# A vision tower in one kernel: zero writes moved behind the pixel transposes, weight means taken off TensorE, and q formed transposed in the linear attention

## The chip, the core and the metric

The kernel runs on one core of a Trainium2 chip. The metric is the device time of one execution in microseconds (us). A core has TensorE (PE, with PEld for its weight loads), VectorE (DVE), ScalarE (ACT), GpSimd (POOL) and SyncE (SP); SP, ACT and POOL issue DMAs.

## The reference

Four images of 3 x 224 x 224 are cut into patches of 8 x 8, 784 per image, each a row of 192 values. A tokenizer and two layers follow, all in fp32 with rows of 256 values:

```python
# tokenizer
tokens = layernorm(patches, ln1_g, ln1_b) @ W1 + b1
tokens = layernorm(tokens, ln2_g, ln2_b)
tokens = concatenate([tokens, tokens, tokens], axis=1)       # 3 x 784 tokens
h1 = silu(layernorm(tokens @ Wp1 + bp1, lnp_g, lnp_b)); h = h1 @ Wp2 + bp2
# layer 0: attention over the images, then 6 experts, the best two of each token
# layer 1: linear attention on x = layernorm(h)
qkv = x @ W_qkv + b_qkv; q, k, v = split(qkv, 3)
q = q - mean(q); k = k - mean(k)
q2 = q*q; k2 = k*k
k2 = l2_normalize(k2 / (sum(k2) + 1e-7), axis=tokens)
q2 = l2_normalize(q2 / (sum(q2) + 1e-7), axis=channels)
kv = einsum('bnc,bnd->bcd', k2, v)
h = h + (v + einsum('bnc,bcd->bnd', q2, kv) / sqrt(N)) @ W_out + b_out
# then 4 small experts and a shared one, the best two of each token
```

## The kernel before

The token rows come three times over, so the kernel works on 784 per image and writes each row three times: 28 tiles of 112 rows (`TT`) in all. h stays in SBUF. The tile framework places the waits; blocks in `tc.manual_schedule` keep the written order on the engines named there, elsewhere a scheduler orders the instructions of each engine. PSUM has seven rotating buffers (`ps_tile`).

**The front (L93 to L575).** DVE sets constants: base0, table, blk and shift for the placing of tokens on experts (L119 to L138, some 70 small memsets and an add), and zeros in the rows of img behind the pixels (L228). TensorE transposes table to tcol (L142). POOL issues the small loads (bp1, the rows of stage); SP and ACT issue W1, Wp1, the four images into img (L224) and the attention's weights. Then POOL clears `nothing` (L252) and SP writes it 40 times to the DRAM buffers xrows and yrows (L256), whose unused rows must be zero. Each hardware DMA takes one of eight semaphore slots in turn and waits for the slot's last user. `tok` is a pool that is closed after the tokenizer (L575); the memory of its tiles is used again by kq, mT and later by the experts' buffers, which wait for the last use of what lay there.

`first_layers` (L376) folds the weights: W1 times the first gain, less its mean over the 192 values of a patch (`without_mean`, L366: a product with a matrix of ones, then DVE), the bias row b1, both put in the order of the transposed pixels by `perm` and `srow` (L404, L408) to give Wall; then the same for Wp1 (W2), and the product of both (L422 to L437). For seven groups of four patch columns `patch_stds` (L440) forms variances on DVE and a root on ACT, which goes into img as a row behind the pixels, and `turn_patches` (L351) transposes pixels with 32 small products for each of two halves, copied to pT by ACT. A last product gives ev; the transposed stage gives cols (L503), the columns of all biases and gains. `first_rows` (L508, products at L517) and `tokenize` follow, then attention (L1086 on) and the experts of layer 0 (L1256 to L1506), whose blocks are read from xrows and written to yrows, with hb as hidden tile.

**The linear attention (L1380 to L1800).** A unit is 4 or 3 tiles of one image; there are eight. `centred_weights` (L623) takes the means out of the q and k columns of Wqkv. For unit u, `x_t` transposes the normalised rows to lxT, `q_k` (L1604) forms q and k of each tile together in a product of 512 columns, adds the bias on DVE (L1624), squares both on ACT in place with sums, and squares q again for the fourth powers (L1629). `scales` (L1637) forms both norms; q is scaled on DVE (L1653), k on ACT (uk). `fold` sums squares of uk. `q_t` (L1671) transposes q. `k_x` (L1676) forms uk^T x of an image, `g_t` and `kv_out` bring it to kvo. `rows_out` (L1728) adds x Wvo + q kvo to h, where Wvo is Wv W_out from `layer1_weights` (L639), called in unit 1 (L1780). Within `q_k`, `stats_one` and `normalise` prepare the rows of the next unit: they add the experts' rows (ys, gathered from yrows by POOL) to h and normalise it.

Of the kernel before, what the change touches and what calls it, by code (L numbers as in the profile page):

```python
# [37 lines left out]
CH = 3  # L38
# [22 lines left out]
def tile_vit_tower(ctx: ExitStack, tc: tile.TileContext, a: dict, out: bass.AP):  # L61
# [57 lines left out]
    base0 = const.tile([TT, E0], F32, tag="base0", name="base0")  # L119
    for e in range(E0):  # L120
        nc.vector.memset(base0[:, e : e + 1], float(CAP * e))


    NQ = QMAX * E0
    table = const.tile([1, 4, NQ], F32, tag="table", name="table")
    for q in range(QMAX):
        nc.vector.memset(table[:, 0, q * E0 : (q + 1) * E0], float(BLK * q))
    by_e = table.rearrange("r k (q e) -> r k q e", e=E0)
    for e in range(E0):
        for k, v in ((1, CAP * e - DUMMY), (2, EW * e), (3, D * e)):  # L130
            nc.vector.memset(by_e[:, k, :, e], float(v))
    nc.vector.tensor_tensor(table[:, 1, :], table[:, 0, :], table[:, 1, :], ALU.add)
    blk = const.tile([NQ, NBLK], F32, tag="blk", name="blk")
    for i in range(NBLK):
        nc.vector.memset(blk[:, i : i + 1], float(i))
    shift = const.tile([1, 3, NBLK], F32, tag="shift", name="shift")
    nc.vector.memset(shift, 0.0)
    nc.vector.memset(shift[:, 0, :], float(DUMMY))  # L138
    tcol = const.tile([NQ, 4], F32, tag="tcol", name="tcol")
    pt = ps_tile("ptable")  # L140
    for k in range(4):
        nc.tensor.transpose(pt[:NQ, k : k + 1], table[:, k, :], ident[:1, :1])  # L142
    nc.vector.tensor_copy(tcol, pt[:NQ, :4])

# [21 lines left out]
    tokp = tok.enter_context(tc.tile_pool(name="tok", bufs=1))  # L166
    bp1 = tokp.tile([TT, D], F32, tag="bp1", name="bp1")
# [39 lines left out]
    WID = HP * PATCH  # L207
    CY = CH * PATCH
    img = tokp.tile([TT, 32, WID], F32, tag="img", name="img")
# [18 lines left out]
    nc.vector.memset(img[:, CY:, :], 0.0)  # L228
# [22 lines left out]
    nothing = tokp.tile([P, 8 * D], F32, tag="nothing", name="nothing")  # L251
    nc.gpsimd.memset(nothing, 0.0)  # L252
    for r in range(0, XROWS, 8 * P):
        n = min(8, (XROWS - r) // P)
        for rows_ in (xrows, yrows):
            nc.sync.dma_start(  # L256
                out=rows_[r : r + n * P, :].rearrange("(p k) d -> p (k d)", k=n),
                in_=nothing[:, : n * D],
            )

# [86 lines left out]

    pT = tokp.tile([P, 2, NI * HP, HP], F32, tag="pT", name="pT")
# [17 lines left out]
    def without_mean(w, n, dim):  # L366

        pm = ps_tile("pmean")[:n, :D]
        for i in range(2):
            nc.tensor.matmul(pm, allones[:n, :n], w[:, i, :], start=(i == 0), stop=(i == 1))  # L370
        for i in range(2):
            nc.vector.scalar_tensor_tensor(
                w[:, i, :], pm, -1.0 / dim, w[:, i, :], ALU.mult, ALU.add
            )

    def first_layers():  # L376
# [14 lines left out]
        W2 = tokp.tile([P, 2, D], F32, tag="W2", name="W2")  # L391
        for i in range(2):
            nc.vector.tensor_scalar(W1g[:, i, :], W1[:, i, :], g1(i), None, ALU.mult)
        without_mean(W1g, KP, PD)
# [5 lines left out]
        nc.vector.tensor_tensor(b1, pw, b1, ALU.add)  # L400
# [10 lines left out]
        for c in range(2):  # L411
            nc.vector.tensor_scalar(W2[:, c, :], Wp1[:, c, :], g2(c), None, ALU.mult)
        for c in range(2):
            nc.vector.tensor_copy(
                bb[:, c, :], gb[:, 6 + c : 7 + c].to_broadcast([P, TT])
            )
        without_mean(W2, P, D)
# [8 lines left out]
        pw = ps_tile("pbw2")[:TT, :D]  # L426
        for c in range(2):
            nc.tensor.matmul(pw, bb[:, c, :], Wp1[:, c, :], start=(c == 0), stop=(c == 1))
        nc.vector.tensor_tensor(bp1, pw, bp1, ALU.add)
# [7 lines left out]
        nc.vector.tensor_copy(Wall[:, :, D:], pp)  # L437
        return Wall
# [42 lines left out]
    with tc.manual_schedule(engines={mybir.EngineType.DVE, mybir.EngineType.PE}):  # L481
        nc.vector.memset(srow, 0.0)
        nc.vector.memset(srow[:, SROW : SROW + 1], 1.0)
        nc.vector.memset(perm, 0.0)
        nc.vector.tensor_reduce(mod4, by4.rearrange("p j b -> p b j"), AX.X, ALU.add)
        nc.vector.tensor_reduce(div4, by4, AX.X, ALU.add)
        by_x = ident[:KP, :KP].rearrange("p (y x c) -> p x c y", x=PATCH, c=CH)
        for half in range(2):
            for i in range(2):
                nc.vector.tensor_copy(  # L490
                    perm[:, half, i, :, :CY].rearrange("p g (c y) -> p g c y", c=CH)[
                        :, :, :, 4 * half : 4 * (half + 1)
                    ],
                    by_x[:, 4 * i : 4 * (i + 1)],
                )
# [7 lines left out]
        nc.vector.tensor_copy(cols, pc[:, :nrows])  # L503
# [71 lines left out]
    tok.close()  # L575

# [62 lines left out]
    def layer1_weights():  # L639
# [8 lines left out]
        nc.vector.tensor_copy(WvT, pt)  # L648
        Wvo = w1p.tile([P, 2, D], F32, tag="Wvo", name="Wvo")
# [8 lines left out]
        bvs = w1p.tile([P, 2, P], F32, tag="bvs", name="bvs")  # L658
        for k in range(2):
            nc.vector.tensor_copy(bvs[:, k, :], col("bv", k).to_broadcast([P, P]))  # L660
# [724 lines left out]


# [35 lines left out]

    def stats_one(u, j):
# [4 lines left out]
        for k in range(2):  # L1428
            nc.vector.scalar_tensor_tensor(
                h[:, t, :], ys[u][:, j, k, :], wk[:, k, t : t + 1], h[:, t, :],  # L1430
                ALU.mult, ALU.add,
            )
        if j == 0:
            st = small.tile([TT, GT, 6], F32, tag="st", name="st")
            mv = small.tile([TT, GT, 2], F32, tag="mv", name="mv")
            stats[u] = st, mv
# [43 lines left out]
    with tc.manual_schedule(engines={mybir.EngineType.DVE, mybir.EngineType.SP}):  # L1480
        own_weights(NEARLY)
        turned(NEARLY)
        for i in range(NEARLY, NBLK + 1):
# [8 lines left out]
            if i == NEARLY + 1:  # L1492
                centred_weights()
            for u in range(3):
                if i - 1 == after[u]:
                    fetch(u)
# [105 lines left out]
    sumsof = {}  # L1602

    def q_k(u, j0, j1):  # L1604

        n = units[u][2]
        xT = xTs[u]
        if j0 == 0:
            qks[u] = lin.tile([TT, GT, 2 * D], F32, tag="qk", name="qk")
            sumsof[u] = (  # L1610
                small.tile([TT, GT, 2], F32, tag="ss", name="ss"),
                small.tile([TT, GT], F32, tag="s4", name="s4"),
            )
        qk = qks[u]
        ss, s4 = sumsof[u]
        junk = lin.tile([TT, D], F32, tag="junk", name="junk", bufs=1)
        for j in range(j0, min(j1, n)):
            pqk = ps_tile("pqk")[:TT]
            for c in range(2):
                nc.tensor.matmul(  # L1620
                    pqk, xT[:, c, cut(j, 1)], Wqkv[:, c, : 2 * D],
                    start=(c == 0), stop=(c == 1),
                )
            nc.vector.tensor_tensor(qk[:, j, :], pqk, bqkv[:, : 2 * D], ALU.add)  # L1624

            for i in range(2):
                half = qk[:, j, i * D : (i + 1) * D]
                nc.scalar.activation(half, half, AF.Square, accum_out=ss[:, j, i : i + 1])  # L1628
            nc.scalar.activation(junk, qk[:, j, :D], AF.Square, accum_out=s4[:, j : j + 1])  # L1629
            if u:  # L1630
                stats_one(u + 1, j)
        if j1 >= n and u:
# [3 lines left out]

    def scales(u):  # L1637

        b, j0, n = units[u]
        qk = qks[u]  # L1640
        ss, s4 = sumsof.pop(u)

        nc.vector.tensor_scalar(ss[:, :n], ss[:, :n], 1e-7, None, ALU.add)
        nc.scalar.activation(s4[:, :n], s4[:, :n], AF.Sqrt, bias=zero[:TT])
        nc.vector.scalar_tensor_tensor(
            ss[:, :n, 0], ss[:, :n, 0], 1e-12, s4[:, :n], ALU.mult, ALU.max
        )
        nc.vector.reciprocal(ss[:, :n], ss[:, :n])
        uk = uks[u] = lin.tile([TT, GT, D], F32, tag="uk", name="uk", bufs=3)
        sq = lin.tile([TT, GT, D], F32, tag="sq", name="sq", bufs=1)  # L1650
        for j in range(n):
            nc.scalar.activation(uk[:, j, :], qk[:, j, D:], AF.Copy, scale=ss[:, j, 1:2])
            nc.vector.tensor_scalar(  # L1653
                qk[:, j, :D], qk[:, j, :D], ss[:, j, 0:1], None, ALU.mult
            )
# [14 lines left out]

    def q_t(u):  # L1671
        n = units[u][2]
        qT = qTs[u] = lin.tile([P, 2, GN], F32, tag="lqT", name="lqT", bufs=3)
        transposed(qks.pop(u), n, lambda c, pt: copy_out(qT[:, c, : n * TT], pt))
# [53 lines left out]
    def rows_out(u):  # L1728
        b, j0, n = units[u]
        xT, qT, kvo = xTs.pop(u), qTs.pop(u), kvos[b]  # L1730
        for two in halves(range(n)):
            pm = ps_tile("pout")[:TT].rearrange("p (t d) -> p t d", t=2)
            for i, j in enumerate(two):
                for c in range(2):
                    nc.tensor.matmul(  # L1735
                        pm[:, i, :], xT[:, c, cut(j, 1)], Wvo[:, c, :],
                        start=(c == 0), stop=False,
                    )
                for c in range(2):
                    nc.tensor.matmul(  # L1740
                        pm[:, i, :], qT[:, c, cut(j, 1)], kvo[:, c, :],
                        start=False, stop=(c == 1),
                    )
# [154 lines left out]
```

## Time and profile before

| | |
|---|---|
| median of three runs | 810.28 us (808.37 to 810.49) |
| the profiled execution's own time | 810.54 us |
| its span, first to last instruction | 808.8 us |
| mean granted TensorE clock | 0.966 |
| busy: PE, PEld, DVE, ACT, POOL | 739.7, 501.2, 504.0, 334.1, 131.0 us |
| front up to the copy of cols (L503) | 51.4 us |
| linear attention, first q and k product to the start of the last stage | 502.7 to 669 us |
| DMA q1: packets, MB | 50832, 80.52 |

Times within the profile count from the span's start. In the page's second part each digit is a tenth of busy share in one of 40 slices of 20.2 us. The profile calls each pass of a product a record: an fp32 product shows as two records with two weight loads, a transpose as one. A timeline row gives start, length, engine, line, operation, tile written and tiles read, the number of records, and the idle time before it with what ended it; "issue" means that nothing in the profile explains the wait. In a table of stretches, the columns are the stretch, its length, busy time of PE, PEld, DVE, ACT and POOL with the number of records, the granted clock, the DMA engines' share and GB/s. The chain of waits lists pieces of the chain that ended last: start, length, engine, tile, line, records.

### The profile page before, as it was taken

To read this page: it belongs to the slowest core of one execution; us is meant where nothing else is said; L and a number is where in the kernel's file an instruction comes from. 1 tells how busy PE (TensorE), PEld (TensorE's weight loads), DVE (VectorE), ACT (ScalarE), POOL (GpSimd) and SP (SyncE) were. 2 spreads that over 40 slices of the span, in tenths; PEclk is the share of its full clock that TensorE was granted. 3 is DMA by queue.
4 is the path that set the end of the run, shared out by engine and by line. 5 is a ranking of instruction groups with operands and counts; after the bars stand their busy time and mean duration, and the time that the engine had idled before them with its cause. 6 is when DMAs were issued, how large, how long until landed. Compare 5 with 4: busy or idle time off the path is not lost. (4 is left out here: it accounts for less than half of the span.)

```text
span 808.8 us, 10871 instructions
## 1 busy us (share of the span) xinstructions
PE 739.7 (91%) x3524; PEld 501.2 (62%) x3524; DVE 504.0 (62%) x1618; ACT 334.1 (41%) x789; POOL 131.0 (16%) x148
## 2 busy tenths in 40 slices
PE   5779996999788887999999999799999999999996
PEld 3645554555555655887888887475776775555553
DVE  4618776586767986546445746699975655554441
ACT  0326776355376475443222322527544503222221
POOL 4100000000006350760012030775000000000000
PEclk9889997999999988999999999899999999999999
DMA  8999991000002167442334334232000003333333
GB/s 204 371 419 421 420 420 46 1 0 1 1 0 63 36 225 237 143 147 92 105 97 132 94 109 128 85 87 69 1 1 1 1 20 89 90 94 94 94 91 90
DMA packets 58183, 97.39 MB, mean 120 GB/s; under 512 B 14519, under 2 KB 48494, under 8 KB 53262
## 3 DMA queue, kind: packets, MB, share of 16 engines
q1 hardware_dynamic: 50832, 80.52, 28.9%
q0 software_dynamic: 6112, 14.01, 6.0%
q10 hardware_dynamic: 1182, 2.16, 1.1%
q8 instruction: 28, 0.46, 0.2%
q14 instruction: 29, 0.24, 0.1%
HBM read 30.93 MB, written 65.74 MB: 120 GB/s over the span
## 5 line engine op out<-in xcount | busy, mean ns | idle before, releaser
L947 POOL DMA_INDIRECT xrows<-xn,pos x56 | 59.8, 1068 | 274.6 <-ACT kq L711 233.3
L1415 POOL DMA_INDIRECT ys<-yrows,pos x56 | 57.2, 1021 | 141.9 <-DMA yrows<-yb 125.8
L1219 PE MATMUL pb<-xTb,own 128*128 128x256 f32 x240 | 58.8, 389 | 3.8 <-DVE r L810 1.6
L1225 ACT ACTIVATE hb<-pb,own 128x256 f32<-128x256 f32 x74 | 35.1, 475 | 56.2 <-PE pb L1219 47.8
L1219 PE MATMUL pb<-hb,own 128*128 128x256 f32 x240 | 57.1, 380 | 0.3 <-DVE hb L1227 0.3
L1236 PE MATMUL pyb<-own,hb 128*128 128x256 f32 x240 | 57.0, 380 | 0.2 <-ACT hb L1225 0.2
L1219 PEld LDWEIGHTS pb<-xTb,own 128*128 128x128 f32 x240 | 44.6, 194 | 12.5 <-ACT hb L1225 1.9
L517 PE MATMUL pw<-Wall,pT 128*112 128x512 f32 x112 | 51.0, 610 | 0.0
L1620 PE MATMUL pqk<-Wqkv,lxT 128*112 128x512 f32 x112 | 49.7, 594 | 0.5 <-ACT lxT L81 0.5
L1236 PEld LDWEIGHTS pyb<-own,hb 128*128 128x128 f32 x240 | 45.4, 190 | 6.7 <-ACT hb L1225 0.6
L1219 PEld LDWEIGHTS pb<-hb,own 128*128 128x128 f32 x240 | 43.3, 190 | 5.9 <-DVE hb L1227 0.9
L300 PE MATMUL pt<-ident,xn 112*128 112x112 f32 x224 | 34.6, 286 | 12.5 <-DVE xn L540 6.8
L309 PE MATMUL pe<-xT,eW 128*128 128x448 f32 x112 | 45.2, 546 | 0.0
L1242 DVE TENSOR_TENSOR yb<-pyb,eb 128x512 f32<-128x512 f32 x30 | 20.7, 691 | 39.2 <-PE pyb L1236 38.8
L1209 ACT COPY xTb<-ptb 128x512 f32<-128x512 f32 x30 | 17.5, 584 | 64.0 <-PE ptb L1205 64.0
L300 PEld LDWEIGHTS pt<-ident,xn 112*128 112x128 f32 x224 | 27.0, 151 | 26.9 <-ACT xn L824 9.5
L1227 DVE TENSOR_SCALAR hb<-pb,own 128x256 f32<-128x256 f32 x46 | 22.1, 481 | 29.5 <-PE pb L1219 29.5
L517 PEld LDWEIGHTS pw<-Wall,pT 128*112 128x112 f32 x112 | 20.1, 182 | 26.2 <-issue 22.9
L320 PE MATMUL pwo<-Wo,oT 128*112 128x256 f32 x112 | 29.0, 413 | 7.5 <-DVE oT L776 6.7
L736 DVE SCALAR_TENSOR_TENSOR prod<-kq 128x784 f32<-128x784 f32 x32 | 30.3, 969 | 7.4 <-ACT kq L711 5.2
L1620 PEld LDWEIGHTS pqk<-Wqkv,lxT 128*112 128x112 f32 x112 | 19.3, 177 | 24.8 <-issue 23.0
L1628 ACT ACTIVATE qk<-qk 112x256 f32<-112x256 f32 x56 | 22.8, 407 | 27.7 <-DVE qk L1624 25.2
(360 smaller groups left out, 1502.6 us busy)
## 6 DMA issues: line engine op xcount, KB each, us to landing
xrows<-nothing SPq DMA_DIRECT2D x19, 1024.0 KB, 20.2
yrows<-nothing SPq DMA_DIRECT2D x19, 1024.0 KB
out_dram<-h SPq DMA_DIRECT2D x26, 336.0 KB, 3.8
xb<-xrows SPq DMA_DIRECT2D x30, 256.0 KB, 2.7
yrows<-yb SPq DMA_DIRECT2D x30, 256.0 KB, 2.2
ew<-in_L_ffn_expert_w_dram SPq DMA_DIRECT2D x6, 768.0 KB, 11.4
wb<-wd SPq DMA_DIRECT2D x28, 112.0 KB, 3.5
img<-in_x_dram SPq DMA_DIRECT2D x2, 588.0 KB
```

What stands on the lines that cost most here:

```text
L300: nc.tensor.transpose(pt[:, j * TT : (j + 1) * TT], xn[:, j, c * P : (c + 1) * P], ident[:TT, :TT])
L309: nc.tensor.matmul(pm[: wcols.stop - wcols.start, :n], w[:, c, wcols], xT(c), start=(c == 0), stop=(c == chunks - 1),)
L320: nc.tensor.matmul(pm[:, i, :], xT(c, t), w[:, c, :], start=(c == 0), stop=(c == chunks - 1))
L517: nc.tensor.matmul(pm, pTf[:, c, cut(t0 + j, 1)], Wall[:, c, :], start=(c == 0), stop=(c == 1))
L736: nc.vector.scalar_tensor_tensor(prod, qTs[s][:, o, :], 1.0, kT[:, o, t * SEQ : (t + 1) * SEQ], ALU.mult, ALU.mult, accum_out=atts[s][:, o ...
L947: put = nc.gpsimd.indirect_dma_start(out=xrows[:, :], out_offset=bass.IndirectOffsetOnAxis(ap=pos[:, k, t0 + j : t0 + j + 1], axis=0), in_ ...
L1219: nc.tensor.matmul(pm, wm[:, c, o * P : (o + 1) * P], src[:, c, :], start=(c == 0), stop=(c == 1),)
L1225: nc.scalar.activation(dst[:, o, :], pm, AF.Relu, bias=b)
L1236: nc.tensor.matmul(pm[:, t, :], src[:, c, t * P : (t + 1) * P], wm[:, c, :], start=(c == 0), stop=(c == 1),)
L1415: got = nc.gpsimd.indirect_dma_start(out=y[:, j, k, :], out_offset=None, in_=yrows[:, :], in_offset=bass.IndirectOffsetOnAxis(ap=pos[:, k, ...
L1620: nc.tensor.matmul(pqk, xT[:, c, cut(j, 1)], Wqkv[:, c, : 2 * D], start=(c == 0), stop=(c == 1),)
L1628: nc.scalar.activation(half, half, AF.Square, accum_out=ss[:, j, i : i + 1])
```

## The change

In the front: img lies first in its pool, and POOL clears the rows behind the pixels. base0, table, blk and shift are set by POOL after the block of `first_layers`; table's transposes stand behind the tokenizer. `nothing` is cleared behind that block too, and each write of zeros waits for the copy of cols. The mean over a patch's values is now in `perm` (1/192 taken from every used entry); the mean of W1's rows over the 256 outputs is formed by a sum along the free axis and taken off with the gain in one instruction, b1's mean likewise, which takes the place of the product of ones for Wp1; and the bias product for bp1 stands last.

In the linear attention: q is formed transposed (`q_of`), one product per 128 channels and unit with the unit's lxT moving; ACT squares it with its bias into lqT and squares it again (q4). `norms` sums q4 over the channels with a matrix of ones of 32 columns, a copy and a small product turn the sums into columns, and the reciprocal root rq scales the rows at the end, in `rows_out`. Wvo takes the place of v's columns in Wqkv, and k is formed beside x Wvo in one product of 512 columns (`k_of`), whose second half goes to h at once; only unit 0 forms k alone, since Wvo is made behind it. WvT is copied by ACT.

```diff
+    img = tokp.tile([TT, 32, WID], F32, tag="img", name="img")
+    nc.gpsimd.memset(img[:, CY:, :], 0.0)
...
-    nc.vector.memset(img[:, CY:, :], 0.0)
...
-    def without_mean(w, n, dim):
-        pm = ps_tile("pmean")[:n, :D]
-        for i in range(2):
-            nc.tensor.matmul(pm, allones[:n, :n], w[:, i, :], start=(i == 0), stop=(i == 1))
...
+        nc.vector.tensor_reduce(m1, W1, AX.X, ALU.add)
+        nc.vector.tensor_scalar(m1, m1, 1.0 / D, None, ALU.mult)
         for i in range(2):
-            nc.vector.tensor_scalar(W1g[:, i, :], W1[:, i, :], g1(i), None, ALU.mult)
-        without_mean(W1g, KP, PD)
+            nc.vector.tensor_scalar(
+                W1g[:, i, :], W1[:, i, :], m1[:, i : i + 1], g1(i), ALU.subtract, ALU.mult
+            )
...
-        without_mean(W2, P, D)
...
+        nc.vector.memset(perm[:, :, :, :, :CY], -1.0 / PD)
...
-        nc.vector.tensor_copy(cols, pc[:, :nrows])
+        turned = nc.vector.tensor_copy(cols, pc[:, :nrows])
+
+    nothing = tokp.tile([P, 8 * D], F32, tag="nothing", name="nothing")
+    nc.gpsimd.memset(nothing, 0.0)
+    for r in range(0, XROWS, 8 * P):
...
+            tc.add_manual_dep(
+                put.ins, turned.ins.name,
...
+        nc.gpsimd.memset(base0[:, e : e + 1], float(CAP * e))
...
-        nc.vector.tensor_copy(WvT, pt)
-        Wvo = w1p.tile([P, 2, D], F32, tag="Wvo", name="Wvo")
+        nc.scalar.copy(WvT, pt)
+        Wvo = Wqkv[:, :, 2 * D :]
...
+    def k_of(u):
...
+            for j in two:
+                if lw:
+                    pk = ps_tile("pk")[:TT]
+                    for c in range(2):
+                        nc.tensor.matmul(
+                            pk, xT[:, c, cut(j, 1)], Wqkv[:, c, D:], start=(c == 0), stop=(c == 1)
+                        )
+                    nc.vector.tensor_tensor(kr[:, j, :], pk[:, :D], bqkv[:, D : 2 * D], ALU.add)
+                    ht = h[:, b * TPI + j0 + j, :]
+                    nc.vector.tensor_tensor(ht, pk[:, D:], ht, ALU.add)
+                nc.scalar.activation(
+                    kr[:, j, :], kr[:, j, :], AF.Square, accum_out=ss[:, j : j + 1]
+                )
...
+    def q_of(u):
...
+        for o in range(2):
+            pq = mm_t(
+                n * TT, Wqkv, slice(o * P, (o + 1) * P), lambda c: xTs[u][:, c, : n * TT], "pq1"
+            )
+            nc.scalar.activation(qT[:, o, : n * TT], pq, AF.Square, bias=bq[:, o : o + 1])
+        nc.scalar.activation(q4[:, :, : n * TT], qT[:, :, : n * TT], AF.Square)
+
+    def norms(u):
...
+                nc.tensor.matmul(
+                    pg[32 * j : 32 * (j + 1), :], ones32, q4[:, c, cut(j, 1)],
+                    start=(c == 0), stop=(c == 1),
+                )
+        qn = small.tile([P, TT], F32, tag="qn", name="qn", bufs=2)[: 32 * n]
+        nc.scalar.copy(qn, pg)
...
+        nc.scalar.activation(r[:, :n], pr, AF.Sqrt, bias=zero[:TT])
+        nc.vector.tensor_scalar(r[:, :n], r[:, :n], 1e-19, None, ALU.max)
+        nc.vector.reciprocal(r[:, :n], r[:, :n])
...
+            pq = mm_rows(two, lambda c, j: qT[:, c, cut(j, 1)], kvo, "pqo")
+            for i, j in enumerate(two):
+                nc.vector.scalar_tensor_tensor(
+                    ht[:, i, :], pq[:, i, :], r[:, j : j + 1], ht[:, i, :], ALU.mult, ALU.add
+                )
...
+            k_of(u)
...
+            q_of(u)
+            norms(u - 1)
+            squares[u] = scales(u)
```

## The prediction

> **What bounds the kernel now.** I read the page's 40 slices first, then TensorE's own timeline over the first 52 us, then a table of busy time and granted clock by stretch, then the waits of SP's queue, and last the chain of waits for the durations in the linear attention. The page:
>
> ```profile
> PE   5779996999788887999999999799999999999996
> DMA  8999991000002167442334334232000003333333
> ```
>
> TensorE is at nine tenths or more in most slices; it is below in slices 0 to 2 (to about 60 us), and in slices 1 to 5 the DMA engines are full. Those slices hold the zero writes to xrows and yrows. TensorE's timeline (start, length, then the idle time before it):
>
> ```profile
> 24.98 1.22 PE L356 MATMUL ptp<-ident,img 112*32 112x112 f32 x38
> 28.28 3.77 PE L356 MATMUL ptp<-ident,img 112*32 112x112 f32 x136 [2.08 <-ACT img L452]
> 35.36 6.05 PE L356 MATMUL ptp<-ident,img 112*32 112x112 f32 x128 [3.31 <-issue]
> 42.93 3.33 PE L356 MATMUL ptp<-ident,img 112*32 112x112 f32 x128 [1.51 <-issue]
> 49.95 0.74 PE L356 MATMUL ptp<-ident,img 112*32 112x112 f32 x18 [3.69 <-issue]
> 51.11 15.68 PE L517 MATMUL pw<-Wall,pT 128*112 128x512 f32 x32
> ```
>
> Three stops wait for nothing that the profile shows, and they stand exactly 128 passes apart, that is 256 records with their weight loads. The page's DMA part lists instruction queue q8 with 28 packets and 0.46 MB, 16.4 KB a packet, or 64 bytes for each of 256 instructions. So TensorE waits for its code: the time from resume to resume is 7.57 and 7.02 us, while 128 passes need 3.33 us at full clock. The code block is queued behind zero writes, each with 20.2 us from issue to landing. The stretches (PE busy, four others, then the clock):
>
> ```profile
> 32.00:35.40 3.40, 0.09 (x8) 0.04 (x4) 3.26 (x18) 0.69 (x2) 0.00 (x0) 0.83 1.01 419
> 35.40:41.40 6.00, 6.00 (x128) 5.83 (x128) 1.78 (x10) 2.24 (x6) 0.00 (x0) 0.52 1.01 418
> 43.00:46.30 3.30, 3.25 (x128) 3.07 (x128) 0.00 (x0) 1.94 (x4) 0.00 (x0) 1.00 1.01 420
> 51.10:55.00 3.90, 3.90 (x6) 1.51 (x6) 0.49 (x3) 0.43 (x2) 0.00 (x0) 0.56 1.01 418
> ```
>
> After the two stops over 3 us the granted clock is 0.52 and 0.56: the same 128 passes take 6.05 instead of 3.33 us, and six passes of L517 take 3.90. The DMA share is 1.01 throughout. Before all this TensorE has only 16.6 us of work in its first 25 us. The waits of SP's queue give the arrival of the images:
>
> ```profile
> SPq L249 <- DMA img<-in_x_dram: 2.6, 1, 2.6
> ```
>
> L249 is issued at 19.38 the moment its queue slot's predecessor, the last image block, has landed. The images are complete at 19.4 us.
>
> **The front, part by part.** *DVE's memsets and the weight means.* 71 DVE instructions move to GpSimd (base0, table, blk, shift, and img's 1.55 us), some 4.0 us of the DVE line that ends at 7.5 us with the copies of gb; a strided memset of perm (0.4, near L484's 0.48) comes in. So gb is ready near 4, W1 (issued 1.48, 2.8 us to landing) near 4.5. The means become a free-axis sum (0.6 us for 96x512, near the rows of L393) and a constant in perm, so both pmean products go (1.99 and 2.07 us of TensorE, with DVE's 0.75 and 0.76 between). What is left is a chain: pbw 1.86, pwc 3.78, bias product 1.22, Wall copy 0.69, pwct 1.06, WcT 0.59, pw 2.75, pbw2 1.91. The row mean of b1 (three small DVE steps, about 1.1) lies beside pwc. From 4.5 this ends at 18.4, with hand-overs near 19. Before it was 24.98. So the images (19.4) and the weights arrive together, and the pixel transposes start at 19.4 instead of 24.98.
>
> *The transposes.* Before, DVE's statistics began at 25.70 and TensorE resumed after the first square root at 28.28, 2.58 later (table load 1.28 in it). From 19.4: 22.0. The remaining 410 passes at 3.33 us per 128 are 10.7: 32.7. DVE's seven groups of 1.64 us end at 30.9, ACT's 14 copies of 0.54 and 7 roots of 0.30 fit, so TensorE sets the pace. The two last products and the copy of cols followed in 0.8: cols is ready at 33.5, before at 51.43. That is 17.9 us, and the cold stretch from 51.1 to 55.0 (44% of 3.9) is 1.7 more: 19.6.
>
> This assumes that code now arrives in time. [...] 8.5 us of stops plus 2.7 and 1.7 of half clock stand in the rows. [...] with the queues empty the nearest landings are 2.8 us (W1) and 2.7 (a 256 KB block of xb), both under 3.33. Bounds: no stop; or three stops of 4 us (the old 7.3 less 3.33) with half clock, 14 us lost.
>
> *The zeros.* 41.4 MB at 420 GB/s are 99 us; they ran from 23.4 to 123.4 and now run from 33.6 to about 134. They no longer lie on the transposes, but fully on L517, where 256 instructions take 30 us and more, so a 7 us fetch is hidden, as it was from 55 to 123. Who waits for their end: before, the first write of mT (138.39) listed all eight queues of the zeros. In the changed program mT waits for none; the first write of kq lists queue counts that belong to the loads of the start, and the zeros are waited for only by the first scatter (246.1 before), by the first write of hb (320.1), and on SP by the expert weights behind them (291.4). Even 24 us earlier, all lie 85 us or more behind 134: cost 0. If that cover were missing and kq waited, it would be 134 against 142.2-19.6=122.6, 11 us.
>
> *GpSimd.* img's memset (1.6, near L252's 1.82) goes ahead of its DMA issues; the last stage load moves from 19.4 to 21, landing 5 to 11 us later, at the latest 32, just ahead of its reader at 33. The 68 small memsets run between 25 and 30. The four transposes of table go into a TensorE gap of 6.82 us at 123. Cost 0; bounds 0 and 2.
>
> **The linear attention.** From 503 to 669 TensorE is the bound (122.8 of the last 123.6 us busy). Durations from the chain of waits:
>
> ```profile
> 625.02 5.15 PE pqk L1620 x12
> 630.17 0.77 PE pt L300 x8
> 638.02 3.02 PE ps L309 x8
> 661.74 0.86 PE pout L1735 x4
> 667.26 0.52 PE pgate L1559 x16
> ```
>
> A pass is 0.429 us at 512 columns, 0.378 at 448, 0.215 at 256, 0.097 for a transpose, 0.033 for a 32-row product; by columns 0.283 at 336. Before: 112 passes pqk 48.1, 224 pout 48.2, 56 transposes of q 5.4: 101.7. After: k with xWvo 96 passes of 512, 41.2; unit 0's k and its xWvo 32 of 256, 6.9; q transposed 32 of 448 and 32 of 336, 21.2; q kvo 112 of 256, 24.1; norms 112 small ones and 16 more, 4.5: 97.9. So TensorE saves 3.8.
>
> DVE loses L1624 19.1, L1653 8.4, L1746 9.9, its lqT copies 4.4 and L1645 1.2: 43.0. It gains 48 adds of 0.42, 4 of 0.685, 28 scaled adds of 0.45, and 16 small steps of 0.17: 38.2. ACT loses 28 squares with their accumulator reads twice over and 3.9 of copies, about 37, and gets 16 squares of lqT (0.55 to 0.63) and 8 double ones (0.8 to 1.1): 17. Neither becomes the bound, though DVE stays at 0.75 to 0.8 of TensorE.
>
> *The start of it.* TensorE stood 5.77 us on WvT:
>
> ```profile
> 513.40 0.60 PE L644 MATMUL pwv<-ident,Wqkv 128*128 128x128 f32 x4
> 519.77 3.78 PE L653 MATMUL pwvo<-Wout,WvT 128*128 128x256 f32 x8 [5.77 <-DVE WvT L648]
> ```
>
> and then ran eight passes in 3.78 instead of 1.72. DVE's copy stood behind steps of the next unit that waited for gathers. Now ACT makes it, behind unit 0's squares: 4 of 0.6, two of lqT 0.63, 4 uk and 4 sq of 0.4, one of 1.1, near 8 us, from 505: WvT near 513.5, TensorE idle there about 3.4 in two pieces. I take 2 saved, bounds 4 saved and 4 lost. Norms: q4 on ACT, product, copy qn on ACT, product, root: each has a unit's time (18 us) except the first, and other products stand between; 1 us lost. Sum: -5, bounds -9 and +4. Elsewhere pbq's four tiny products: 0.2.
>
> **Sum.** -19 (19.6 less half a microsecond for fetches) and -5 give -24 on the profiled execution's own 810.54 (span 808.8): 786.5. The median of the runs, 810.28, stands 0.26 below it: 786.3.
>
> **The rivals.** *Code is still late, or the images are.* The loads of the first 20 us hold a block up, or the fetch itself needs 5 us: two or three stops of 2 to 4 us and half clock. For it: no row shows a fetch on empty queues. Against it: 2.8 us landings. Front -10, time 795. *The linear attention gives nothing.* DVE's two adds per tile and statistics come in a burst and TensorE waits for PSUM: 0 to +3, time 792 to 795. *Slower than before: the norms.* [...] if ACT's queue holds q4 or qn back in each of 8 units, everything behind waits. From 3 us a unit the whole gain is gone; at 4, with 2 us of half clock behind it, 48 us are lost: 835. Against it: ACT is busy under half the time and its work falls. *It doesn't do what it says:* kq waits for the zeros after all: 797.
>
> **How the numbers follow.** Both parts work, 779 to 791: 0.67. Front short: 0.15. Linear attention flat or worse, still faster: 0.13. Slower or equal: 0.05. The range 779 to 798 covers front -21 to -10 and linear -9 to +4, not both bad ends at once. A measurement tells 0.3% (2.4 us) from no change: faster 0.95, same 0.02, slower 0.03.
>
> **What would show it.** In the profile after: the transposes of pixels begin near 19.4 with no "issue" stops over 0.5 us and clock 1.00; cols is copied at 32 to 35; the zeros' first issue follows it and the last bytes move near 134 with kq's first write near 122; pwvo waits under 4 us for WvT; TensorE ends the linear attention some 5 us faster than 166. Wrong would be stops 128 passes apart without zeros, kq at 134, or TensorE waiting for qn or rq in each unit.

## The result: 796.8 us, about half of the forecast gain

| | before | after |
|---|---|---|
| median of four runs | 809.33 us (807.63 to 810.49) | 796.77 us (796.40 to 801.06) |
| the profiled execution's own time | 810.54 us | 796.94 us |
| its span | 808.8 us | 795.2 us |

The ratio is 0.9867 with a 95% interval of 0.9836 to 0.9897, which makes 10.8 us less (8.3 to 13.3); the medians lie 12.6 apart. The forecast was 24 less, 786.3. The time lies inside the range, but near where the rivals had put it that let one half of the change bring nothing.

The page of after, busy share of TensorE and of the DMA engines in 40 slices:

```profile
PE   6899969997998789989999998988999999999996
DMA  8399998000011393442242224321000013323333
```

The full DMA slices have moved behind slice 1, and TensorE's first slices are fuller; but slices 24, 26 and 27 (477 to 497 and 517 to 557 us) stand at eight tenths, where before had a single seven in slice 25. That is the linear attention's start. I laid the two timelines of TensorE beside each other, stage by stage (the first pass of each stage, for cols the end of its copy, in us; "shift" is after less before):

| stage | before | after | shift | change of shift | forecast |
|---|---|---|---|---|---|
| copy of cols (L503, L466) | 51.43 | 36.29 | -15.1 | -15.1 | -17.9 |
| first pkv of attention | 139.17 | 122.12 | -17.05 | -1.9 | -1.7 |
| first product of the linear attention | 501.38 | 485.42 | -15.96 | +1.1 | +0.2 |
| first pe of the last stage | 664.08 | 650.40 | -13.68 | +2.3 | -5 |
| end of the span | 808.8 | 795.2 | -13.6 | 0 | 0 |

So the front did what was forecast, 2 us short. The linear attention gained nothing: it takes 2.3 us longer. (It runs from 501.38 to 664.08 before; the 502.7 to 669 given further up take in a piece of the last stage.) The old form of it takes 161.2 to 162.7 us in the four profiles that have it in this order (before, e1, e5, e6 below), the new form 165.0 and 165.2 (after, e2), so the sign is not one profile's chance. TensorE's timeline of the front in after (start, length, then the idle time and what ended it):

```profile
19.54 1.24 PE L321 MATMUL ptp<-ident,img 112*32 112x112 f32 x38 [1.37 <-DMA rw<-in_L_ffn_router_w_dram]
22.95 11.76 PE L321 MATMUL ptp<-ident,img 112*32 112x112 f32 x406 [2.18 <-ACT img L414]
35.13 0.42 PE L321 MATMUL ptp<-ident,img 112*32 112x112 f32 x4 [0.42 <-issue]
35.98 13.99 PE L515 MATMUL pw<-Wall,pT 128*112 128x512 f32 x32
```

The transposes begin at 19.54 and run through 406 passes; one stop of 0.42 is left of 8.5 us. L515 needs 13.99 us for the 32 passes that took 15.68. The stretches of after (length, busy PE, PEld, DVE, ACT, POOL, granted clock, DMA share, GB/s):

```profile
22.95:26.00 3.05, 3.04 (x84) 3.05 (x88) 2.91 (x16) 1.39 (x4) 3.05 (x69) 0.66 0.62 49
26.00:29.00 3.00, 3.00 (x106) 3.00 (x102) 2.90 (x15) 1.64 (x5) 0.48 (x4) 0.77 0.02 5
29.00:32.00 3.00, 3.00 (x130) 2.95 (x126) 2.17 (x14) 2.58 (x8) 0.00 (x0) 1.00 0.00 0
```

Here the mean clock is 0.66 and 0.77 over 6 us with no full DMA queue near: the half clock can stand behind the wait for the first root too. It need not: before waits as long for its root (2.08 us, here 2.18) and keeps the full clock. In pieces of 3.41 us (length, busy PE, granted clock, DMA share, GB/s), first after, then before:

```profile
20.53:23.94 3.41, 1.23 (x49) 1.00 1.05 257
23.94:27.36 3.42, 3.42 (x84) 0.50 0.26 11
27.36:30.77 3.41, 3.41 (x151) 1.00 0.02 5
```

```profile
24.04:27.45 3.41, 2.17 (x43) 1.00 1.01 351
27.45:30.87 3.42, 2.56 (x96) 1.00 0.99 417
```

In after the wait lies whole in one such piece, in before it is parted between two. The last section says why the pieces are cut so.

The linear attention in two stretches, up to unit 2's first k product and from there on; first before, then after:

```profile
501.38:545.37 43.99, 36.87 (x145) 25.20 (x143) 35.15 (x100) 18.69 (x69) 31.02 (x31) 0.92 0.30 85
545.37:664.08 118.71, 117.88 (x527) 82.15 (x527) 88.40 (x270) 57.80 (x208) 11.44 (x11) 1.00 0.05 13
```

```profile
485.42:533.56 48.14, 41.65 (x179) 29.55 (x177) 29.81 (x87) 16.41 (x47) 33.24 (x33) 0.86 0.29 84
533.56:650.40 116.84, 113.92 (x532) 73.27 (x533) 85.44 (x287) 49.91 (x143) 10.72 (x9) 1.00 0.04 11
```

Busy time times clock gives the work at full clock, as an estimate: 36.87 x 0.92 + 117.88 = 151.8 before, 41.65 x 0.86 + 113.92 = 149.7 after. So three terms make the 2.3: passes -2.1; half clock 2.9 before and 5.8 after, +2.9; idle time 7.95 before and 9.41 after, +1.5. What TensorE waited for in after, over the whole linear attention (in total, times, longest):

```profile
PE pq L1707 <- ACT q L1697: 3.1, 2, 1.6
PE pn L1756 <- DVE acc L1749: 1.9, 1, 1.9
PE pwvo L671 <- ACT WvT L666: 1.5, 1, 1.5
PE pk L1662 <- ACT lxT L81: 1.2, 2, 1.0
PE pkvo L1795 <- ACT gT L1786: 0.8, 2, 0.7
```

The one wait of 5.8 us for WvT has become several smaller ones. ACT's timeline shows how the two at unit 0 come about, for q4 (tile q in the rows) and for WvT:

```profile
492.08 0.63 ACT L1696 ACTIVATE lqT<-pq,bq 128x448 f32<-128x448 f32 x1
492.62 0.50 ACT L1735 ACTIVATE uk<-kr,ss 112x256 f32<-112x256 f32 x1
493.01 0.94 ACT L1697 ACTIVATE q<-lqT 128x896 f32<-128x896 f32 x1
493.85 0.50 ACT L1735 ACTIVATE uk<-kr,ss 112x256 f32<-112x256 f32 x1
494.25 1.32 ACT L1737 ACTIVATE sq<-uk 112x256 f32<-112x256 f32 x4
495.48 0.56 ACT L666 COPY WvT<-pwv 128x512 f32<-128x512 f32 x1
```

The transposes of Wv had begun at 491.88, but their copy to WvT is last in a queue that has no gap: TensorE stands 1.52 us for q4 and 1.50 for WvT, and pwvo behind them takes 3.78 us at half clock, as in before.

### The profile page after: what moved, and what is told of

Same layout as the page of the kernel before. It is cut to its first block, busy times and chain, and to the rows that moved or that the text cites. A ratio compares the mean times of both kernels' runs of the same rounds, so it can differ in the third digit from the quotient of the medians.

```text
span 795.2 us, 10867 instructions
## 1 busy us (share of the span) xinstructions
PE 734.5 (92%) x3560; PEld 493.0 (62%) x3560; DVE 491.1 (62%) x1552; ACT 327.6 (41%) x708; POOL 136.7 (17%) x219
## 4 chain that ended last, share of the span: by engine, by line
PE 78%; DVE 10%; ACT 6%; DMA 3%; issue 2%; SPq 0%; ACTq 0%; DVEq 0%
PE pb L1234 12%; PE pyb L1251 6%; PE pw L515 6%; PE pkv L273 6%; PE pe L273 5%; PE pk L1662 5%; PE ps L273 4%; PE pwp L284 3%; PE pqo L284 3%; PE pt L264 3%; PE ps L1924 3%; PE pq L273 2%; PE pukx L1769 2%; DMA img<-in_x_dram 2%; PE ps L1918 2%
## 5 line engine op out<-in xcount | busy, mean ns | idle before, releaser
L515 PE MATMUL pw<-Wall,pT 128*112 128x512 f32 x112 | 49.3, 593 | 0.0
L1662 PE MATMUL pk<-Wqkv,lxT 128*112 128x512 f32 x96 | 42.7, 596 | 1.2 <-ACT lxT L81 1.2
L515 PEld LDWEIGHTS pw<-Wall,pT 128*112 128x112 f32 x112 | 19.6, 177 | 25.1 <-issue 21.4
L273 PEld LDWEIGHTS pe<-xT,eW 128*128 128x128 f32 x112 | 20.2, 190 | 20.9 <-issue 20.9
L1211 DVE COPY own<-ew 128x1540 f32 x30 | 29.1, 970 | 5.2 <-issue 1.3
```

The lines of the kernel that those rows point to most:

```text
L273: nc.tensor.matmul(pm[: wcols.stop - wcols.start, :n], w[:, c, wcols], xT(c), start=(c == 0), stop=(c == chunks - 1),)
L515: nc.tensor.matmul(pm, pTf[:, c, cut(t0 + j, 1)], Wall[:, c, :], start=(c == 0), stop=(c == 1))
L1211: nc.vector.tensor_copy(w, ewf[0][:, bass.ds(off, EW)])
L1662: nc.tensor.matmul(pk, xT[:, c, cut(j, 1)], Wqkv[:, c, D:], start=(c == 0), stop=(c == 1))
```

## The experiments

The theory after the result: the gain of the change is the front's; the linear attention lost its part at image 0, where nothing stands between the links of a chain that goes from engine to engine, to waits and to the half clock behind them. Rivals: the front spoils something later; DVE or ACT bounds the new form; the new products on TensorE are simply too many. Each ratio below is to runs of the kernel before on the same chip. "Under the full change" and "over e8" compare medians that come in part from different chips, where the kernel before has medians of 808.0 to 809.6, so they are good to some 2 us.

**Each half alone (e1, e2).** The diff is cut in two: the front's edits, and the linear attention's with the bias products.

```diff
e1, on before (and the rest of the front's edits):
-        without_mean(W1g, KP, PD)
...
+            tc.add_manual_dep(
+                put.ins, turned.ins.name,
...
e2, on before (and the rest of the linear attention's edits):
-            q_k(u, 0, 2)
+            k_of(u)
...
+            q_of(u)
+            norms(u - 1)
```

> Only the front of the change (zeros behind the pixel transposes, constants on GpSimd, weight means without products of ones); the linear attention as before. Theory: the whole gain of the change is in the front; cols is copied near 36 and everything behind it shifts by 17, with nothing lost later: 17 us under the kernel before, near 792.5, and so 4 us under the full change. Rival: the 1.1 us that the experts of layer 0 lost in the full change, or more, comes from the front (zeros still being written, constants on GpSimd): then only 13 to 15 us.

> Only the linear attention's part of the change (with its bias products among the experts); the front as before. Theory: this part costs time by itself, 1 us among the experts (the bias products) and 2.3 in the linear attention: 3 us over the kernel before, near 812.5. Rival: what the forecast said, it gains 5 by itself, and the loss in the full change comes from an interplay with the earlier front: near 804.

Measured: e1 793.21 us, ratio 0.9815 (0.9787 to 0.9843), 15 us less (in the rival's 13 to 15, and the interval, 12.7 to 17.2, holds the theory's 17 too); e2 811.71 us, ratio 1.0042 (1.0018 to 1.0066), 3.4 us more, as the theory had it. The halves add up to the whole within the intervals, and the linear attention's half is a loss by itself: the interplay is out. On the experts e1's trace sides with the rival: from the first pkv to the linear attention it takes 363.5 us, after 363.3, before 362.2.

**Zeros or weight means (e5, e6).** e5 moves only the zeros (and img); e6 has the whole front, with the zeros at their old place; so it holds the weight means and the constants moved to GpSimd together, and no run parts these two.

```diff
e5, on before:
-    nothing = tokp.tile([P, 8 * D], F32, tag="nothing", name="nothing")
...
-        nc.vector.tensor_copy(cols, pc[:, :nrows])
+        turned = nc.vector.tensor_copy(cols, pc[:, :nrows])
+
+    nothing = tokp.tile([P, 8 * D], F32, tag="nothing", name="nothing")
...
e6, on e1: the block of nothing and its writes back ahead of h = res.tile
```

> Of the front's change only the place of the zero writes (behind the copy of cols) and the place and clearing of img; weight means by products of ones and the constants of DVE as before, the linear attention as before. Theory (the transposes waited for their code behind the zeros): they begin at 25 as before, the three stops of 8.5 us and the half clock behind them go, cols is copied near 41: 10 to 13 us under the kernel before, near 796. Rival (the time of the start counts, stops come anyway): the stops 128 passes apart stay, and the gain is under 3.

> The whole front of the change except that the zeros are written where they were before (from 23 on); the linear attention as before. Theory: the transposes begin near 19.4, but blocks of code still come 7.0 to 7.6 us apart behind the zeros; only the blocks asked for ahead of the zeros are early: 3 to 6 us under the kernel before, near 804. Rival (the zeros don't matter): 15 to 19 us under it, as with the whole front.

Measured: e5 796.55 us, ratio 0.9852 (0.9835 to 0.9868), 12 us less; e6 802.00 us, ratio 0.9913 (0.9896 to 0.9929), 7 us less, a little over the theory's 3 to 6 and far from the rival's 15 to 19. TensorE's timeline of e5:

```profile
22.66 1.22 PE L346 MATMUL ptp<-ident,img 112*32 112x112 f32 x38
26.83 12.14 PE L346 MATMUL ptp<-ident,img 112*32 112x112 f32 x410 [2.95 <-ACT img L442]
```

and of e6:

```profile
22.93 9.89 PE L331 MATMUL ptp<-ident,img 112*32 112x112 f32 x278 [2.27 <-ACT img L424]
35.38 4.87 PE L331 MATMUL ptp<-ident,img 112*32 112x112 f32 x124 [2.55 <-issue]
42.67 0.60 PE L331 MATMUL ptp<-ident,img 112*32 112x112 f32 x4 [2.33 <-issue]
```

Without zeros in the queue 410 passes run with no stop, with zeros the stops are back, 7.29 us from resume to resume. An earlier start ahead of early zeros still gains 7: 316 passes are done before the first such stop, in before 174. (e5 begins its transposes 2.3 us before the kernel before does, as img's clearing has left DVE; so it is a little more than the zeros.) The two gains, 12 and 7, give 19 and the whole front 15: they overlap, since both lessen the same stops.

**Wv W_out made earlier (e3).** Its transposes, copy and products go among the experts, and unit 0 forms k beside x Wvo.

```diff
             if i == NEARLY + 5:
                 nc.vector.tensor_copy(bq, pbq[:, :2])
+                WvT = turned_v()
+            if i == NEARLY + 7:
+                Wvo = v_out(WvT)
+            if i == NEARLY + 9:
+                bvo, bres = v_bias(bvs)
...
+            lw.extend((Wvo, bvo, bres))
             k_of(0)
...
-            lw.extend(layer1_weights(bvs))
```

> The full change, but Wv is transposed, copied and multiplied with W_out among the experts (three of the blocks behind the bias products) instead of behind unit 0's k and q, so that unit 0 forms k with x Wvo too. Theory: TensorE's waits of 1.52 us for q4 and 1.50 for WvT go, and with them the half clock on pwvo (3.78 instead of 1.9): 3.5 to 5 us under the full change. Rival: ACT's queue of squares and DVE's fold hold TensorE up a little later anyway, at unit 0's norms and at pn, and the gain is 1 us or none.

Measured: 791.14 us (788.07 to 793.06), ratio 0.9774 (0.9735 to 0.9814), 5.6 us under the full change, with runs that scatter over 5 us. The waits at unit 0 are gone, but others come behind them: 1.69 us for g, and in unit 3 1.59 for q4 and 0.95 for lxT, with 12 passes of pk at half clock for 8.45 us instead of 5.3. The size is nearer the theory's (3.5 to 5), the waits that follow are the rival's.

**Unit 2's statistics behind the fold (e4).**

```diff
-            if u == 1:
-                next_stats(u)
...
             fold(u, squares.pop(u))
+            if u == 1:
+                next_stats(u)
```

> The full change, but the statistics of unit 2 are put behind unit 1's last fold on DVE instead of ahead of it. Theory: TensorE's wait of 1.85 us for acc (L1749) goes, and pkvo, which took 3.78 us at half clock behind it, runs in 2: 2 to 3.5 us under the full change. Rival: the rows of unit 2 are now late, TensorE waits for lxT instead: no gain, or a loss of 1 to 2 us.

Measured: 799.05 us, ratio 0.9882 (0.9854 to 0.9910), no gain. TensorE's timeline tells why:

```profile
513.11 0.61 PE L1756 MATMUL pn<-ones,acc 112*128 112x1 f32 x4
520.57 0.47 PE L1783 MATMUL pgT<-ident,g 128*128 128x128 f32 x1 [4.21 <-DVE g L1773]
522.10 0.90 PE L1783 MATMUL pgT<-ident,g 128*128 128x128 f32 x3 [1.06 <-DVE g L1773]
```

The wait for acc is gone, and the statistics now stand ahead of g, one link further on: 4.21 and 1.06 us in place of 1.85. The rival had the right sign, but not the right wait (it named lxT). A new order within DVE did not help while TensorE had nothing else to do.

**Without norms (e7).**

```diff
-        nc.scalar.activation(q4[:, :, : n * TT], qT[:, :, : n * TT], AF.Square)
...
-                nc.tensor.matmul(
-                    pg[32 * j : 32 * (j + 1), :], ones32, q4[:, c, cut(j, 1)],
...
-        nc.scalar.activation(r[:, :n], pr, AF.Sqrt, bias=zero[:TT])
...
+        nc.vector.memset(r[:, :n], 1.0)
```

> The full change without the norms of q: q4, its sums over channels, the copy, the small product and the root are left out, and rows are scaled by 1 (so this part of the computation is changed). Theory: on TensorE the norms cost 1.5 us an image in the steady part, and the waits for q4 at the start and in unit 3 (1.5 and 1.6 us) go with them: 6 to 10 us under the full change. Rival (the norms' passes are hidden in TensorE's waits for others): under 3.

Measured: 790.72 us, ratio 0.9777 (0.9746 to 0.9807), 6 us under the full change, the low end of the theory's 6 to 10 (in unit 3 TensorE now waits 2.30 us for lxT where it waited 0.96). In the steady part, from unit 4's first k product to unit 6's, an image takes 33.47 us against 35.39 with norms and 35.80 in before. So the norms cost 1.9 us an image, 7.7 in four, and the new form without them would be 2.3 us an image under the old; with them it is 0.4 under.

**Image 0 filled (e8, e10).** e8 is e3 with image 0 in the order of the later ones; e10 has this without e3's part.

```diff
         if u == 2:
-            gT = g_t(0)
-            kv_out(0, gT)
-            rows_out(0)
             x_t(2)
         if u < len(units):
             k_of(u)
-        if one_image and b:
+        if one_image:
             gT = g_t(b)
```

> Wv W_out made among the experts as in the run before (e3), and image 0 handled like the later ones: unit 2's rows are transposed and its k and q formed between the products of image 0 instead of behind them. Theory: TensorE's waits at image 0 (1.69 for g, 0.67 for gT, 0.71 for kn and qn) and at unit 3 (1.6 for q4, 0.95 for lxT) are filled, and the half clock behind them goes: 4 to 8 us under e3, near 785. Rival: unit 2's rows hang on DVE (experts' rows to be added, statistics), TensorE waits for lxT instead, and the gain is 2 or less.

> The full change with image 0 handled like the later ones, but Wv W_out behind unit 0 as in the change. Theory: the waits for q4 and WvT behind unit 0 stay (1.5 and 1.5 us, with pwvo at half clock), the others go: 8 to 12 us under the full change and 4 to 6 over e8, near 787. Rival: the wait at unit 0 was what made the later ones (its lateness runs through the chain), so that filling image 0 without it gives 3 us or less.

Measured: e8 781.54 us (780.71 to 782.15), ratio 0.9663 (0.9646 to 0.9679); e10 787.64 us, ratio 0.9734 (0.9713 to 0.9755). e8 is the best kernel of this study, 15 us under the full change and 27 under the kernel before. It is 9.6 under e3, where its theory had said 4 to 8. Its TensorE over the whole linear attention, and all that it waits for there (its lines stand 10 further down):

```profile
487.76:635.06 147.30, 146.38 (x678) 93.53 (x677) 114.19 (x375) 65.04 (x187) 43.44 (x42) 1.00 0.13 37
```

```profile
PE pq L1717 <- ACT kn L1771: 0.4, 1, 0.4
PE pk L1672 <- ACT lxT L81: 0.2, 1, 0.2
PE pws L1625 <- ACT rq L1729: 0.2, 1, 0.2
PE pkvo L1805 <- ACT gT L1796: 0.2, 1, 0.2
```

Idle 0.9 instead of 9.4 us, clock 1.00 instead of 0.96. The passes at full clock are the same: 146.4, and with 3 us of Wv W_out now among the experts 149.4, against 149.7. So the waits and the half clock were all that stood between the full change and a gain. DVE is busy for 114.19 and ACT for 65.04 of these 147.30 us: neither bounds the new form. e10 keeps the waits at unit 0, 1.63 and 1.50, and pwvo at 3.78, and is 6.1 over e8, as its theory had it: the other part of the loss.

**The old form of q in the new order (e9).** e1 with the same two moves as e8.

```diff
+            lw.extend((Wvo, bvo, bres))
             q_k(0, 0, GT)
...
         if u == 2:
-            gT = g_t(0)
-            kv_out(0, gT)
-            rows_out(0)
             x_t(2)
```

> The changed front, and the linear attention in the form of the kernel before (q and k in one product, q scaled by rows and then transposed, x Wvo formed at the end), but with the two moves of e8: Wv W_out among the experts, and image 0 handled like the later ones. Theory: what e8 gained is the order, and the new form of q is worth its steady 0.4 us an image, 1.6 in all: 1 to 3 us over e8, near 783.5. Rival: without the new form DVE and ACT, which get back 43 and 37 us of work, hold TensorE up once its own waits are filled: 6 us or more over e8, near 788 to 792.

Measured: 788.39 us, ratio 0.9747 (0.9726 to 0.9768), 6.9 over e8. The number is the rival's, its mechanism stands only at one place. In the steady part an image takes 35.56 us, 0.4 more than e8's 35.18, and no wait: neither DVE nor ACT binds. But in unit 1 there is this:

```profile
502.86 0.41 PE L264 MATMUL pt<-ident,qk 112*128 112x112 f32 x2 [2.50 <-DVE qk L1672]
```

TensorE stands 2.50 us for the rows of q scaled by DVE, a step that the new form has not, and the mean clock up to unit 3 is 0.96. So of the 6.9 the form's passes are 1.6, this wait with two of 0.2 is 3, and some 2 are half clock (45.19 us at 0.96) and scatter.

## Why the forecast was half right

- *The start of the transposes at 19.4:* right, 19.54.
- *Resume at 22.0:* 22.95. I counted 2.58 us from DVE's statistics; in both kernels the root's table load (1.28 us) stands on ACT behind the first copy of pT, so the time counts from the first transposes: 3.30 before, 3.41 after. A term mis-sized by 0.9.
- *No stops, code in time:* right, and shown by e5 and e6. It was my estimate from the landings of 2.8 and 2.7 us on empty queues. With the zeros moved 0.42 us of stops are left in after and none in e5; behind the zeros of e6 there are two, of 2.55 and 2.33 us.
- *Clock 1.00:* wrong here, 0.66 and 0.77 over 6 us, 1.2 us lost. I took the half clock to go with the stops; it can stand behind the 2.2 us wait for the root as well. This is luck: in e3, with the same code up to there and the same wait (2.20), the clock of 22.95 to 32 is 1.00.
- *The cold stretch of L517, 1.7:* right, 15.68 to 13.99 us.
- *The zeros, cost 0:* right. By the DMA records the last of them end some 12 us later than before, at 134.1, and kq's first copy is made at 125.2 all the same: it doesn't wait for them.
- *Elsewhere 0.2:* 1.1 in attention and the experts. The bias products pbq stand there for 0.6 us, but e1, e5 and e6, which have none, lose 1.0 to 1.6 in the same stretch; the cause stays open.
- *The failed step is the linear attention's -5.* Its three terms: "TensorE saves 3.8" was -2.1, mostly as the norms cost 1.9 us an image where I had put 4.5 + 1 for all; "2 saved" at its start was right for that one place (3.4 us of idling in two pieces forecast, 3.0 measured), but the sum stopped there. I had asked what is late next only for WvT. Behind it TensorE now waited for acc, kn, qn, lxT and, in unit 3, again for q4: idle +1.5 over all where -1 was forecast. And half clock, which I had read off in the front and at pwvo, did not stand in the sum: +2.9, on pkvo above all (3.78 us instead of 1.99). It is not one profile's chance: of this stage's stretches of half clock, the old form has one (before, e1, e5, e6), the new form two (after, e2, e3, e4, e7), until the waits are filled (e10 one, e8 none).
- *The rivals:* "the linear attention gives nothing" came true in size (+2.3, inside its 0 to +3), for another reason than PSUM. "The norms hold every unit back" did not: L1707 waits twice, not in each of eight units.

## What to carry to other kernels

Where a chain passes from engine to engine once, at the head of a pipeline, removing its longest wait moves the loss to the next link: look for other work to put between the links, as the steady part has it (e8), before making any link faster (e4). Where the profile shows half clock behind such a wait, charge that too (here 1.5 us more of waits and 2.9 us more of half clock), and add up short waits that stand close together (1.85, 0.35, 0.36 and 0.67 us in image 0). And a form that saves little in the steady part is not to be sold on its pass count before its small products are priced by a run without them.

## What the runs showed of the hardware

- In the trace's DMA records the first four blocks of TensorE's code (16,384 bytes each) take 0.9 to 1.2 us themselves. Behind the zeros they start 7.5, 7.3 and 7.5 us apart (before) and 8.0, 7.2 and 7.9 (e6), without them 3.4, 3.8 and 4.8 (after), where 128 of the transposes take 3.33 us at full clock. Behind the zeros a block's own transfer is no longer (0.88 to 0.94 us); it comes later.
- In the granted clock of before and of after, the stretches of half clock that end before the kernel does are nine each: four of 3.41 us, four of 6.83 and one of 10.24. Within a profile they begin whole multiples of 3.41 us apart (in after at 23.94, 109.28, 494.98 and 518.88: 25, 138 and 145 times 3.4133 behind the first); the pieces shown here and above are cut on these marks. What the same wait cost differed from run to run: in e1, e3 and e4, whose code is the same up to there, 16 passes of pwp behind the same wait of 6.57 us took 4.35, 4.78 and 5.66 us, as half clock lasted to 115.91, 116.67 and 118.59: each is 3.6 us and half of what was left of the stretch. In unit 3, after has waits of 1.60 and 0.96 us and e3 of 1.59 and 0.95; only in e3 does half clock follow (after, then e3; length, busy PE, granted clock, DMA share, GB/s):

```profile
542.77:546.18 3.41, 1.81 (x22) 1.00 0.14 44
546.18:549.60 3.42, 2.46 (x17) 1.00 0.26 72
```

```profile
536.51:539.92 3.41, 1.52 (x23) 1.00 0.31 88
539.92:546.75 6.83, 6.17 (x8) 0.50 0.31 90
```

These lengths make 1.4 of the 2.1 us (pwp takes 5.79 us in after, 4.35 in e1) by which profiles of like fronts differ (a shift of 17.05 us in after and 19.2 in e1), so single profiles don't settle smaller differences.
- In after, 3.78 us of pwvo at half clock stand behind two gaps of TensorE of 1.52 and 1.50 us with 0.6 us of work between them, and 3.78 us of pkvo behind gaps of 1.85, 0.35, 0.36 and 0.67 in image 0. Half clock cost the changed linear attention 2.9 us more than the old one, and in e8, where 0.9 us of gaps are left, the clock is 1.00. TensorE is busy for 1.50 of the 3.41 us ahead of pwvo's stretch and for 1.20 of those ahead of the one in image 0 (the rows below). Of the pieces of 3.41 us at full clock in this stage, half clock follows those in which TensorE is busy for 0.44 and 0.35 of the time in after and for 0.00 in before; of the others the least busy have 0.53 (after, at 542.77) and 0.54 (before, at 512.14). Over the whole kernel no single share parts them (in after, half clock follows the piece at 242.40 with 0.69 and not the one at 259.46 with 0.47), so this is no rule for other code.

```profile
491.57:494.98 3.41, 1.50 (x22) 1.00 0.35 98
494.98:501.81 6.83, 5.71 (x13) 0.50 0.30 85
515.46:518.88 3.42, 1.20 (x17) 1.00 0.27 74
518.88:525.70 6.82, 5.81 (x16) 0.50 0.30 84
```
